# Graph layer on one core: gathers listed ahead in fours, steps joined, a new first part, placing one turn earlier

## The chip, the core and the metric

The kernel runs on one core of one Trainium2 chip. TensorE (PE; its weight loads are PEld), VectorE (DVE), ScalarE (ACT), GpSimd (POOL) and SyncE (SP) each work through a queue of their own in order and wait for one another by semaphores. The metric is the device time of one execution in microseconds.

## What is computed

One layer of a graph network over 12500 nodes of 128 features and 400000 edges, sorted by their target node `dst`; the edge type is 0 or 1:

```python
Xs = X[src]
m_data = Xs @ W_data.T + b_data
m_ctrl = Xs @ W_control.T + b_control
msg = jnp.where((edge_types == 0)[:, None], m_data, m_ctrl)
agg = jax.ops.segment_sum(msg, dst, num_segments=X.shape[0])
out = agg + (X @ W_self.T + b_self)
return jax.nn.relu(out)          # x = layernorm(x + this)
```

## The kernel before

The sums over edges are taken of the rows of x, apart by type, and multiplied by the weights afterwards. x is split into three bf16 parts that add up to the f32 value (`x3` in SBUF, `rows3` in DRAM, 3 x 128 columns a row).

The edges are 3125 chunks of 128. They make 25 groups of 125 chunks, and a group has four parts (`NE`). Each part is a run of 11 or 12 chunks that are **gathered** (kind "p") and a run of 20 chunks that are **picked** (kind "e").

- *Gathered*: for each chunk POOL gathers 128 rows of `rows3` by an indirect DMA (L700, tile `msg`), and TensorE adds them to their nodes by three products with a 0/1 matrix `psel` and one product that counts (L658, L712). `msg` has 24 buffers (`AHEAD`).
- *Picked*: the rows come from SBUF. Each step brings 25 lots (`q`) of 128 rows. For each, four TensorE products with 0/1 columns (`pick`) copy rows of `x3` into the PSUM tile `got` (L732); two lots share a `got`, of which there are two. ScalarE copies it to `emsg` (L743, five buffers). Three products with `esel` then add the lot to its nodes (L658), and one counts (L761). Rows that don't fit go through one small indirect gather, tile `last` (L747), and an extra copy (L756).

`picked(w)` is one of 100 **steps**, seven units long: unit t < 6 makes the got of lots 4t to 4t+3, counts and adds the lots of the unit before; the seventh adds the last lots, runs what is tiled there, and accumulates. `esel` is made by VectorE in three goes (`choose`, two buffers). Where a step's sums end, `accumulate` (L682) loads a start column `place_i` into a register and adds the PSUM tile `sums` to `acc` in SBUF (L688). `sums` has two buffers, shared by gathered and picked.

What a step picks is worked out ahead. `give_slots(w+2)` runs within step w: the matrix `O` (VectorE), a product `before` (L537), `ranks` and `rank_matrix` (VectorE, up to `rv`), then `put` (L601, 20 products) and `spread` (copy `cell`, write `there`, and load it to all partitions as `pick`, on SP's queue) in unit 5, and `turn_codes` and `keep_codes` (L621, L489; copies L631, L496, L498, and L500, which makes `idx` for `last`) in unit 6. `pick_matrix` (L643) compares `pick` in place. `prep_e` and `prep_p` ready the index data of the next group; `finish` multiplies by the weights, normalises and writes out once a group is complete.

`merged` sorts units of several streams by a fraction of the step, and within the lists a scheduler still moves an instruction of an engine's queue ahead of others where it expects it to be ready earlier. The gathers of `msg` are issued where a chunk is used, and that scheduler moves them forward as far as the 24 buffers go.

The first part loads and splits x (`split_units`: L246 to L249), loads the weights on ScalarE's queue (L274, L275), builds tables, works out `near`, `place_i` and the start nodes `node0` from the first edges of all windows (`first_i`, eight small loads), and makes the slots of steps 0 and 1.

Of the kernel before, what the change touches and what calls it, by code (L numbers as in the profile page):

```python
# [46 lines left out]
AHEAD = 24  # L47
# [101 lines left out]
def short_path(ctx, tc, const, ident, eps, wT, brow, bad, x, src, dst, etype, ws, bs, out):  # L149
# [49 lines left out]
    first_i = keep.tile([1, NG, NWIN], I32, name="first_i")  # L199

    def load_first(kind):
        for i, (k, _, c, _) in enumerate(windows(0)):
            if k == kind:
                nc.sync.dma_start(
                    out=first_i[:, :, i:i + 1],
                    in_=dst.rearrange("(o g e) -> o g e", o=1, g=NG)[:, :, c * P:c * P + 1],
                )
# [65 lines left out]
    for i, (w, b) in enumerate(zip(ws, bs)):  # L273
        nc.scalar.dma_start(out=wn[:, i, :], in_=w)  # L274
        nc.scalar.dma_start(out=brow[:, i, :], in_=b.rearrange("(o d) -> o d", o=1))  # L275
# [61 lines left out]
    halves = tmp.tile([1, 2, NG * NWIN], I32, name="halves")  # L337
    nc.vector.memset(x3[:, NBLK - 1], 0.0)
    first = first_i.rearrange("o g w -> o (g w)")
    nc.vector.tensor_single_scalar(halves[:, 0, :], first, 7, op=OP.logical_shift_right)  # L340
    nc.vector.tensor_single_scalar(halves[:, 1, :], first, 127, op=OP.bitwise_and)
    halves_b = tmp.tile([1, 2, NG * NWIN], BF, name="halves_b")
    nc.vector.tensor_copy(halves_b, halves)
    fin0 = ps1.tile([P, 512], FP, name="fin")
    for i in range(2):
        nc.tensor.matmul(fin0[:, :NG * NWIN], scale[:, i, :], halves_b[:, i, :], start=(i == 0), stop=(i == 1))
    node0 = keep.tile([P, NG, NWIN], FP, name="node0")
    nc.vector.tensor_copy(node0, fin0[:, :NG * NWIN].rearrange("p (g w) -> p g w", w=NWIN))
    near = keep.tile([rows_p, NG], FP, name="near")
    from_i = tmp.tile([rows_p, 1], I32, name="from_i")  # L350
    from_f = tmp.tile([rows_p, 1], FP, name="from_f")
    nc.gpsimd.iota(from_i, pattern=[[0, 1]], base=-PAD, channel_multiplier=DPC)
    nc.vector.tensor_copy(from_f, from_i)
    for k in range(1, NE):
        ge = raw[f"ge{k}"] = tmp.tile([rows_p, 1], FP, name=f"ge{k}")
        nc.vector.tensor_scalar(
            ge, from_f, float(DPC * PB * k - PAD), float(-DPC * PB), op0=OP.is_ge, op1=OP.mult
        )
    for k in range(1, NE):
        nc.vector.tensor_add(from_f, from_f, raw.pop(f"ge{k}"))  # L360
    nc.vector.tensor_scalar(near, near_i, from_f, None, op0=OP.add)
    place = tmp.tile([1, 2, NG, NWIN], FP, name="place")
    ref = tmp.tile([1, NG, NE, 2], I32, name="ref")
    nc.gpsimd.iota(ref, pattern=[[GN, NG], [0, NE], [-PAD, 2]], base=PAD - M0, channel_multiplier=0)
    ref = ref.rearrange("o g e k -> o g (e k)")
    least = tmp.tile([1, NG, NWIN], FP, name="least")
    for i, (_, _, c, _) in enumerate(windows(0)):
        nc.vector.memset(least[:, :, i:i + 1], float(max(0, c * DPC - PAD)))
    nc.vector.tensor_tensor(place[:, 0], first_i, ref, op=OP.subtract)
    nc.vector.tensor_tensor(place[:, 1], place[:, 0], least, op=OP.max)  # L370
    nc.vector.tensor_scalar(place[:, 1], place[:, 1], float(R - WMAX), None, op0=OP.min)
    place_i = keep.tile([1, NG, NWIN], I32, name="place_i")
    nc.vector.tensor_copy(place_i, place[:, 1])
    nc.vector.tensor_tensor(place[:, 0], place[:, 0], place[:, 1], op=OP.not_equal)
    nc.vector.tensor_reduce(worst[0:1, 2, 0:1], place[:, 0].rearrange("o g w -> o (g w)"), AX.X, OP.max)

    wps = ps1.tile([P, 512], FP, name="fin")
    for i in range(3):
        nc.tensor.transpose(wps[:, i * D:(i + 1) * D], wn[:, i, :], ident)
    nc.scalar.copy(wT, wps[:, :3 * D].rearrange("p (i d) -> p i d", d=D))  # L380
# [36 lines left out]
    def prep_p(g):  # L417
# [6 lines left out]
        def first():  # L424
            nc.vector.tensor_copy(sf, s)
            nc.vector.tensor_scalar(rel, d, near[:, g:g + 1], None, op0=OP.subtract)
            codes["n", g] = code_of(rel, t, PW, 0, "p")
# [11 lines left out]
    def prep_e(g):  # L439
# [3 lines left out]
        for i in range(NE):  # L443
            cs = slice(i * EC, (i + 1) * EC)
            nc.vector.tensor_scalar(rel[:, cs], d[:, cs], node0[:, g, 2 * i + 1:2 * i + 2], None, op0=OP.subtract)
# [59 lines left out]
    def give_slots(w):  # L505
# [128 lines left out]
        s["tiled"] = {5: [put, spread], 6: [turn_codes, keep_codes]}  # L634
# [47 lines left out]
    def accumulate(g, i, ps, wide, width):  # L682

        begin_acc(g)
        with tc.issue_after(added[-2].ins) if len(added) > 1 else ExitStack():
            at = nc.vector.value_load(place_i[0:1, g, i:i + 1], min_val=0, max_val=R - WMAX)
        win = acc[g][:, :, bass.ds(at, width)]
        added.append(nc.vector.tensor_add(win, win, ps[:, :4 * wide].rearrange("p (a w) -> p a w", w=wide)[:, :, :width]))  # L688

    def gathered(g, i):  # L690
# [7 lines left out]
        def chunk(c):  # L698
            msg = mp.tile([P, 3 * D], BF, name="msg")
            nc.gpsimd.indirect_dma_start(  # L700
                out=msg, out_offset=None, in_=rows3[:, :],
                in_offset=bass.IndirectOffsetOnAxis(ap=codes["p", g][0][:, i * PB + c:i * PB + c + 1], axis=0),
            )
# [7 lines left out]
            add_rows(rows, msg, sel, c == 0, c == n - 1)  # L711
# [6 lines left out]
    def picked(w, tiled):  # L718
# [46 lines left out]

        def unit(t):

            if t < turns:
                for q in range(t * per, (t + 1) * per, pair):
                    rows(q)  # L770
            if t == 0:
                choose(0)
            if t == 1:
                choose(8)
                spare_rows()
            if t == 3:
                choose(16, 9)
            if 0 < t < turns:
                for q in range((t - 1) * per, t * per if t < turns - 1 else NQ):
                    count(q)  # L780
            if t < turns:
                for u in tiled.get(t, []):
                    u()
            if t == turns - 1:
                last_rows()
            if t > 0:
                for q in range((t - 1) * per, t * per if t < turns else NQ):
                    add_rows(cells_of(s["ps"], EW, 0), s["msg"].pop(q), s["sel"][q], False, q == NQ - 1)
            if t == turns:
                for u in tiled.get(t, []):  # L790
                    u()
                accumulate(g, 2 * i + 1, s["ps"], EW, EW)

        turns = (NQ - 1) // per
        return evenly([lambda t=t: unit(t) for t in range(turns + 1)])
# [106 lines left out]

    prep_e(0)
    merged(evenly(all_slots(0) + all_slots(1)), evenly(split_units))
# [5 lines left out]
    mp = ctx.enter_context(tc.tile_pool(name="msg", bufs=AHEAD))  # L910
# [6 lines left out]
    for u in prep_p(0):  # L917
        u()

# [8 lines left out]

    for w in range(pairs):
# [4 lines left out]
        if i == 2 and g + 1 < NG:  # L934
# [9 lines left out]
        if w + 3 < pairs:  # L944
            more += [(0.55, lambda: [u() for u in begin_slots(w + 3)])]
        merged(
            chunks.pop(w, []),
            picked(w, tiled),
# [3 lines left out]
            evenly(rest),  # L952
# [3 lines left out]
        for p in closed.pop(w, []):  # L956
# [5 lines left out]
            if gp == NG - 1 and ip in soon:  # L962
                rest += finish(gp, soon[ip])
    for u in rest:
        u()
# [158 lines left out]
```

## Time and profile before

| | us |
|---|---|
| median of 9 runs | 2422.44 |
| lowest, highest | 2406.81, 2442.39 |
| the profiled execution | 2432.58 |
| its span, first to last instruction | 2430.8 |
| mean granted clock of TensorE, as a share of full | 0.900 |

The page cuts the span into 40 slices. Each digit is the busy share in tenths; PEclk is the granted clock in tenths:

```profile
PE   0468887888878887887778777787887878888878
DVE  6747676666666676676666666666766665666753
ACT  3435555555545554555545554455554544555535
POOL 0356565666556666566556565566665565666561
PEclk9869899898888989999889998889998898999989
```

The first slice and a half are the first part; the steps run from about 77 us on, with the opening of the main loop in slices two and three; they are alike until the end.

Costly groups beside those shown further on (line, engine, operation; busy us, mean ns of one | idle of the engine before them, and who ended most of it):

```profile
L700 POOL DMA_INDIRECT msg<-rows,pidx x1125 | 1270.5, 1129 | 871.4 <-PE sums L658 430.9
L732 PE MATMUL got<-x,pick 128*32 128x384 bf16 x9800 | 669.4, 358 | 262.7 <-ACT emsg L743 179.0
L658 PE MATMUL sums<-esel,emsg 128*128 128x176 bf16 x7200 | 757.1, 257 | 49.9 <-issue 48.1
L463 DVE TENSOR_TENSOR esel<-code_col,code 128x1408 bf16<-128x1408 bf16 (+1 forms) x300 | 275.0, 917 | 372.7 <-PE sums L658 259.9
```

"issue" is idle time with no wait that the profile shows; "remote", or "another core or an unknown queue", is a semaphore event that it can't put down to an engine.

### The profile page before, as it was taken

To read this page: it belongs to the slowest core of one execution; us is meant where nothing else is said; L and a number is where in the kernel's file an instruction comes from. 1 tells how busy PE (TensorE), PEld (TensorE's weight loads), DVE (VectorE), ACT (ScalarE), POOL (GpSimd) and SP (SyncE) were. 2 spreads that over 40 slices of the span, in tenths; PEclk is the share of its full clock that TensorE was granted. 3 is DMA by queue.
4 is the path that set the end of the run, shared out by engine and by line. 5 is a ranking of instruction groups with operands and counts; after the bars stand their busy time and mean duration, and the time that the engine had idled before them with its cause. 6 is when DMAs were issued, how large, how long until landed. Compare 5 with 4: busy or idle time off the path is not lost.

```text
span 2430.8 us, 70786 instructions
## 1 busy us (share of the span) xinstructions
PE 1883.0 (77%) x28867; PEld 1380.9 (57%) x28867; DVE 1584.9 (65%) x4224; ACT 1231.3 (51%) x2322; POOL 1392.3 (57%) x1243
## 2 busy tenths in 40 slices
PE   0468887888878887887778777787887878888878
PEld 0246565656555665665556555565665656666646
DVE  6747676666666676676666666666766665666753
ACT  3435555555545554555545554455554544555535
POOL 0356565666556666566556565566665565666561
PEclk9869899898888989999889998889998898999989
DMA  7423343332333333333333332323323332333331
GB/s 205 143 75 106 93 110 89 96 104 82 100 81 103 105 88 99 106 85 104 102 87 94 88 100 84 104 83 102 104 84 98 87 95 82 104 97 104 83 98 41
DMA packets 185017, 236.73 MB, mean 97 GB/s; under 512 B 80295, under 2 KB 152282, under 8 KB 184682
## 3 DMA queue, kind: packets, MB, share of 16 engines
q0 software_dynamic: 57200, 115.59, 18.3%
q1 hardware_dynamic: 114418, 109.94, 14.5%
q10 hardware_dynamic: 13064, 6.60, 1.0%
q8 instruction: 228, 3.74, 0.7%
q14 instruction: 107, 0.88, 0.1%
HBM read 215.35 MB, written 16.64 MB: 95 GB/s over the span
## 4 chain that ended last, share of the span: by engine, by line
PE 63%; ACT 10%; issue 9%; DVE 7%; another core or an unknown queue 6%; DMA 3%; SPq 1%; POOL 0%; DVEq 0%; ACTq 0%; POOLq 0%
PE sums L658 30%; PE got L732 22%; ACT emsg L743 9%; PE fin L850 3%; PE rk L601 2%; PE sums L761 2%; PE rk L489 1%; PE sums L712 1%; DVE esel L463 1%; DMA xt<-in_x_dram 1%; PE rk L537 1%; DVE pick L643 1%; PE rk L621 0%; PE fin L837 0%
## 5 line engine op out<-in xcount | busy, mean ns | idle before, releaser
L700 POOL DMA_INDIRECT msg<-rows,pidx x1125 | 1270.5, 1129 | 871.4 <-PE sums L658 430.9
L743 ACT CAST emsg<-got 128x768 bf16<-128x768 f32 x1200 | 921.1, 803 | 837.9 <-PE got L732 357.1
L732 PE MATMUL got<-x,pick 128*32 128x384 bf16 x9800 | 669.4, 358 | 262.7 <-ACT emsg L743 179.0
L658 PE MATMUL sums<-esel,emsg 128*128 128x176 bf16 x7200 | 757.1, 257 | 49.9 <-issue 48.1
L658 PEld LDWEIGHTS <-emsg 128*128 128x128 bf16 x7200 | 587.8, 104 | 221.6 <-issue 217.9
L463 DVE TENSOR_TENSOR esel<-code_col,code 128x1408 bf16<-128x1408 bf16 (+1 forms) x300 | 275.0, 917 | 372.7 <-PE sums L658 259.9
L732 PEld LDWEIGHTS <-pick 128*32 128x32 bf16 x9800 | 244.8, 98 | 446.6 <-issue 360.2
L658 PE MATMUL sums<-psel,msg 128*128 128x48 bf16 x3375 | 243.0, 188 | 49.3 <-issue 36.5
L658 PEld LDWEIGHTS <-msg 128*128 128x128 bf16 x3375 | 191.5, 100 | 80.2 <-issue 74.1
L688 DVE TENSOR_TENSOR acc<-acc,sums 128x352 f32 (+1 forms) x200 | 94.0, 470 | 160.8 <-PE sums L658 50.7
L712 PE MATMUL sums<-psel,one_col 128*128 128x48 bf16 x1125 | 185.7, 186 | 16.7 <-issue 16.4
L747 POOL DMA_INDIRECT last<-rows,idx x100 | 117.8, 1178 | 139.8 <-DMA pdst<-in_dst_dram 91.8
L761 PE MATMUL sums<-esel,one_col 128*32 128x176 bf16 x2500 | 168.6, 257 | 16.4 <-issue 13.9
L463 DVE TENSOR_TENSOR O<-cell_col,blk 128x2000 bf16<-128x2000 bf16 x100 | 119.3, 1193 | 60.6 <-PE got L732 28.0
L643 DVE TENSOR_SCALAR pick<-pick,lane_f 128x1600 bf16<-128x1600 bf16 x200 | 126.2, 646 | 15.1 <-DMA pick<-there 14.8
L601 PE MATMUL rk<-rv,O 128*128 128x64 bf16 x2000 | 90.3, 198 | 56.0 <-DVE rv L589 35.0
L761 PEld LDWEIGHTS <-one_col 128*32 128x32 bf16 x2500 | 85.0, 105 | 66.6 <-issue 33.5
L712 PEld LDWEIGHTS <-one_col 128*128 128x128 bf16 x1125 | 110.2, 98 | 17.2 <-issue 16.9
L551 DVE TENSOR_TENSOR prod<-O,ahead 128x2000 bf16<-128x2000 bf16 x100 | 119.0, 1190 | 0.0
L547 DVE TENSOR_REDUCE ahead<-rk 128x100 bf16<-128x500 f32 x100 | 67.5, 675 | 76.1 <-PE got L732 50.8
L601 PEld LDWEIGHTS <-O 128*128 128x128 bf16 x2000 | 73.9, 101 | 74.3 <-issue 61.3
L631 ACT CAST code<-rk 128x50 bf16<-128x50 f32 x100 | 20.3, 203 | 184.2 <-PE got L732 81.6
(170 smaller groups left out, 1995.4 us busy)
## 6 DMA issues: line engine op xcount, KB each, us to landing
pick<-there SPq DMA_DIRECT2D x100, 800.0 KB
msg<-rows,pidx POOLq DMA_INDIRECT x1125
rows<-x SPq DMA_DIRECT2D x6, 1344.0 KB
xs<-in_x_dram SPq DMA_DIRECT2D x99, 62.5 KB
out_dram<-h SPq DMA_DIRECT2D x99, 62.5 KB
xt<-in_x_dram ACTq DMA_DIRECT2D x6, 896.0 KB
psrc<-in_src_dram SPq DMA_DIRECT2D x100, 6.0 KB
pdst<-in_dst_dram SPq DMA_DIRECT2D x100, 6.0 KB
```

The source lines that it names most:

```text
L463: nc.vector.tensor_tensor(sel.rearrange("p n (w t) -> p n w t", t=2), col[:rows].rearrange("p (o w t) -> p o w t", o=1, t=2).to_broadcast( ...
L551: nc.vector.tensor_tensor(prod, s["O"], ahead.rearrange("p (o j) -> p o j", o=1).to_broadcast([P, EC, NCELL]), op=OP.mult)
L601: nc.tensor.matmul(s["rk"][:m, :2 * CAP], s["held"][:, c * NCELL:c * NCELL + m], s["rv"][:, c].rearrange("p v r -> p (v r)"), start=(c == ...
L643: nc.vector.tensor_scalar(t, t, lane_f, None, op0=OP.is_equal)
L658: nc.tensor.matmul(out, msg[:, j * D:(j + 1) * D], sel, start=(start and j == 0), stop=stop, skip_group_check=True)
L688: added.append(nc.vector.tensor_add(win, win, ps[:, :4 * wide].rearrange("p (a w) -> p a w", w=wide)[:, :, :width]))
L700: nc.gpsimd.indirect_dma_start(out=msg, out_offset=None, in_=rows3[:, :], in_offset=bass.IndirectOffsetOnAxis(ap=codes["p", g][0][:, i * P ...
L712: nc.tensor.matmul(cnt, one_col, sel, start=False, stop=(c == n - 1), skip_group_check=True)
L732: nc.tensor.matmul(ps[CAP * a:CAP * (a + 1), :], slots[w]["pick"][:, a * NQ + q, :], x3[:, 4 * q + a - a0].rearrange("p j d -> p (j d)"), ...
L743: nc.scalar.copy(msg, ps[:, :, :3 * D])
L747: nc.gpsimd.indirect_dma_start(out=msg[:OVF, :], out_offset=None, in_=rows3[:, :], in_offset=bass.IndirectOffsetOnAxis(ap=slots[w]["idx"], ...
L761: nc.tensor.matmul(cells_of(s["ps"], EW, 1)[CAP * (q % 4):CAP * (q % 4 + 1), :], one_col[:, :CAP], s["sel"][q], start=(q < 4), stop=(q + 4 ...
```

## The change

Constants: gathers come in tiles of four chunks (`SB`), six such tiles (`HOLD`), five of them listed ahead.

```diff
-AHEAD = 24
+SB = 4
+HOLD = 6
+AHEAD = 5
...
+    def fetch():
+        if to_fetch:
+            g, i, c = to_fetch.pop(0)
+            msg = mp.tile([P, SB, 3 * D], BF, name="msg")
+            for k in range(min(SB, PC[i] - c)):
+                at = i * PB + c + k
+                nc.gpsimd.indirect_dma_start(
+                    out=msg[:, k, :], out_offset=None, in_=rows3[:, :],
+                    in_offset=bass.IndirectOffsetOnAxis(ap=codes["p", g][0][:, at:at + 1], axis=0),
+                )
+            fetched.append(msg)
...
         def chunk(c):
-            msg = mp.tile([P, 3 * D], BF, name="msg")
-            nc.gpsimd.indirect_dma_start(
...
-            )
+            if c % SB == 0:
+                fetch()
+                s["msg"] = fetched.pop(0)
...
-    mp = ctx.enter_context(tc.tile_pool(name="msg", bufs=AHEAD))
+    mp = ctx.enter_context(tc.tile_pool(name="msg", bufs=HOLD))
...
+    for _ in range(AHEAD):
+        fetch()
```

The last five stand after `prep_p(0)`, ahead of the first step, so the first two gathers of `last` now follow 20 gathers of `msg`. Since rows are fetched earlier, `prep_p(g + 1)` moves from the step of part 2 to that of part 1, which also holds `prep_e(g + 1)`.

Steps have six units. What was the seventh is `end`, and the next step calls it in its first unit, after its own first got and its first `choose`. The gather of `last` moves from unit 1 to unit 2, and the units of `finish` start at 0.1 of the step.

```diff
+        def add(q0, q1):
+            for q in range(q0, q1):
+                add_rows(cells_of(s["ps"], EW, 0), s["msg"].pop(q), s["sel"][q], False, q == NQ - 1)
...
         def unit(t):
...
+            for q in range(t * per, (t + 1) * per, pair):
+                rows(q)
+            if t in (0, 1):
+                choose(8 * t)
             if t == 0:
-                choose(0)
-            if t == 1:
-                choose(8)
+                ending()
+            if t == 2:
                 spare_rows()
...
+        def end():
+
+            add((turns - 1) * per, NQ)
+            for u in tiled.get(turns, []):
+                u()
+            accumulate(g, 2 * i + 1, s["ps"], EW, EW)
...
-        return evenly([lambda t=t: unit(t) for t in range(turns + 1)])
+        return evenly([lambda t=t: unit(t) for t in range(turns)]), end
...
+        units, ending = picked(w, tiled, ending)
         merged(
             chunks.pop(w, []),
-            picked(w, tiled),
+            units,
...
-            evenly(rest),
+            evenly(rest, 0.1),
```

`put` and `spread` go from the sixth unit to the fifth:

```diff
-        s["tiled"] = {5: [put, spread], 6: [turn_codes, keep_codes]}
+        s["tiled"] = {4: [put, spread], 6: [turn_codes, keep_codes]}
```

First part: `first_i` becomes two tiles, one per kind, and the start nodes need that of "e" alone; the weights and biases are loaded on SP's queue, behind the first loads there; the first piece of x is split ahead of `prep_e(0)`; what works out `near` and `place_i` and turns the weights is one function, listed at 0.97 of the first part.

```diff
-    first_i = keep.tile([1, NG, NWIN], I32, name="first_i")
+    first_i = {k: keep.tile([1, NG, NE], I32, name=f"first_{k}") for k in "ep"}
...
-        nc.scalar.dma_start(out=wn[:, i, :], in_=w)
-        nc.scalar.dma_start(out=brow[:, i, :], in_=b.rearrange("(o d) -> o d", o=1))
+        nc.sync.dma_start(out=wn[:, i, :], in_=w)
+        nc.sync.dma_start(out=brow[:, i, :], in_=b.rearrange("(o d) -> o d", o=1))
...
-    first = first_i.rearrange("o g w -> o (g w)")
+    first = first_i["e"].rearrange("o g w -> o (g w)")
...
+    def places_and_weights():
+        near = raw["near"] = keep.tile([rows_p, NG], FP, name="near")
...
+    split_units.pop(0)()
     prep_e(0)
-    merged(evenly(all_slots(0) + all_slots(1)), evenly(split_units))
+    merged([(0.97, places_and_weights)], evenly(all_slots(0) + all_slots(1)), evenly(split_units))
```

## The prediction

> **What bounds the kernel now.** I read the page first, then the list of waits, then one step boundary in order of time, then stretches with their granted clock. From the page (L743 and L631 are the two copies of ScalarE that matter; behind the bar stands the idle time before them):
>
> ```profile
> span 2430.8 us, 70786 instructions
> ...
> PE 1883.0 (77%) x28867; PEld 1380.9 (57%) x28867; DVE 1584.9 (65%) x4224; ACT 1231.3 (51%) x2322; POOL 1392.3 (57%) x1243
> ...
> PE 63%; ACT 10%; issue 9%; DVE 7%; another core or an unknown queue 6%; DMA 3%; SPq 1%; POOL 0%; DVEq 0%; ACTq 0%; POOLq 0%
> ...
> L743 ACT CAST emsg<-got 128x768 bf16<-128x768 f32 x1200 | 921.1, 803 | 837.9 <-PE got L732 357.1
> ```
>
> No engine is full. TensorE carries 63% of the chain but stands still for 23% of the span; 100 steps share some 2330 us, 23.3 us each. The groups view adds the code copy, and the list of waits says who holds whom (us, times, longest):
>
> ```profile
> L631 ACT CAST code<-rk 128x50 bf16<-128x50 f32 x100 | 20.3, 203 | 184.2 <-PE got L732 81.6 <-PE sums L658 56.8 <-PE rk L489 30.7
> ```
>
> ```profile
> POOL msg L700 <- PE sums L658: 430.9, 301, 13.1
> ...
> ACT emsg L743 <- remote: 199.6, 61, 15.6
> PE got L732 <- ACT emsg L743: 179.0, 213, 16.1
> ```
>
> ScalarE stands 1.84 us per step in front of the code copy; TensorE loses 179 us to emsg copies; the gathers wait for free buffers, and TensorE waits for gathers only 1.2 us in all. One boundary in order of time (start, length, then what; idle time before it in brackets):
>
> ```profile
> 1286.72 1.07 PE L658 MATMUL sums<-esel,emsg 128*128 128x176 bf16 x12
> ...
> 1288.98 0.20 ACT L631 CAST code<-rk 128x50 bf16<-128x50 f32 x1 [2.10 <-PE sums L712]
> ...
> 1289.67 0.80 ACT L743 CAST emsg<-got 128x768 bf16<-128x768 f32 x1 [0.38 <-ACT part L498]
> ...
> 1291.74 0.95 POOL L700 DMA_INDIRECT msg<-rows,pidx  x1 [0.30 <-issue]
> ...
> 1292.99 1.02 POOL L700 DMA_INDIRECT msg<-rows,pidx  x1 [0.30 <-issue]
> ...
> 1293.69 0.31 PE L658 MATMUL sums<-esel,emsg 128*128 128x176 bf16 x2 [0.81 <-issue]
> ...
> 1295.18 0.20 PE L658 MATMUL sums<-psel,msg 128*128 128x48 bf16 x1 [1.15 <-issue]
> ...
> 1295.30 1.50 ACT L743 CAST emsg<-got 128x768 bf16<-128x768 f32 x2 [3.77 <-remote]
> ```
>
> TensorE ends a step with its last sums while ScalarE idles 2.10 us, queued behind a code copy that needs those sums done; only then does it copy the next step's first got. Then TensorE halts twice without a wait (0.81 and 1.15 us), in a run of gathers 1.25 us apart. The stretches show the clock (after the comma: PEclk, DMA share, GB/s):
>
> ```profile
> 1290.70:1300.00 9.30, 6.47 (x83) 4.50 (x79) 4.71 (x9) 3.81 (x5) 4.59 (x5) 0.72 0.39 127
> 1300.00:1308.00 8.00, 7.10 (x125) 4.86 (x125) 6.00 (x20) 4.38 (x6) 5.51 (x5) 0.90 0.20 51
> ```
>
> ```profile
> 106.00:132.00 26.00, 4.89 (x44) 1.97 (x43) 6.31 (x16) 2.10 (x3) 19.90 (x21) 0.57 0.29 76
> ```
>
> The third row is the 24 gathers that open the main loop, in one run: TensorE works 4.89 of 26 us.
>
> **The change part by part**, against the profiled execution's 2432.6 us (span 2430.8 and 1.8 around it), which is 10 us or 0.4% above the median of nine.
>
> A, joined steps. No instruction is added. The last 15 sums of a step, turn_codes and the accumulation move behind the next step's first 16 got. In the order in which the changed instructions stand, two emsg copies come between the last and the code copy in 97 steps, where none did. They need 2 x 0.803 = 1.61 us and fit into the hole of 1.84: 97 x 1.61 = 156 us of copies leave the restart. TensorE can win what it waits for them: 179.0 less the 16.1 of the opening is 163 us, and at the least half of it belongs to the restart (in the step above 0.30 and 0.58 us follow it, 0.71 and 0.19 come later): 81. I take 110, nearer the lower end, since the hole was partly cover for other waits. The later code copies delay idx and the gather of last by a turn; that gather is listed a turn later too, and its rows are used three turns on, so nothing is charged.
>
> B, the clock. A mean of 0.900 between 0.5 and 1.0 (132 to 141 us and 1289 to 1290.7 us show 0.50 and 1.00) is 0.2 x 2430.8 = 486 us at half rate; the stretch from 100 to 141 (0.51, 0.57, 0.50) takes 37, leaving 449, or 4.5 per step, and 9.3 x 0.28 x 2 = 5.2 of it follows the boundary above. At TensorE's share of 77%, half of 449 is 173 us at stake. I take a third, 58 (bounds 0 and two thirds, 115), because the halts in gather runs stay, and slow stretches follow those too. The Trainium skill, TensorE: Matmul & The Clock Gate, "What's actually happening", says that the gate drops to half rate after an idle window of about 3.4 us, and that for modelling the ramp is under 1% of a span. By that 1%, B would be at most 24 us and the sum 102 instead of 136. The rows, with 4.5 us of half rate in each step, say more.
>
> C, first part. VectorE waits 5.46 us for first_i up to 19.07, then works off prep_e and the places; the first split stands at 28.82. Changed, prep_e needs only the first four loads and runs in that hole, and the split stands right behind psf (23.41): up to 5 us. ScalarE's later waits for xt (3.85 and 4.95) may eat it; the six weight issues (0.29 to 0.57 us, 2.4 together) now go ahead of group 1's loads on SP, and bias is needed tens of us later. I take 3 (0 to 5).
>
> D, the opening. Twenty gathers are listed ahead of the first two last: 20 x 1.25 = 25 us later for these, and TensorE needs the first at the end of step 0, now inside step 1. But in that run it works 4.89 of 26 us anyway, and the rest of the run is shorter by as much. Taken 0; bounds -8 and +20.
>
> E, placing a turn earlier. The 20 rk products mostly move in front of 16 got. At four boundaries rv ends 3.5, 2.3, 3.4 and 2.1 us before rk starts; 16 got are 0.83 us: covered. If the cover goes, 0.5 us a step, 50. On SP the write of there and the pick load come earlier, and the load then stands waiting for the step's last got, with index loads, xs and out queued behind it; all waits for pick sum to 14.8 us and for esrc to 9.8. Taken 0, bounds 0 and 50.
>
> F, prep_p a step earlier. Six VectorE operations (204, 277, 277, 280, 210, 274 ns: 1.52 us) join the step that holds prep_e, 25 times: 0 to 38 us; VectorE is 65% busy: 10. Spreading finish from 0.1 moves nothing that is waited for.
>
> G, a new wait. The next step's first counts reuse the bank that the accumulation (0.47 us) empties, and the joined accumulation comes close in front of them. Between stand turn_codes, 7 products for spares, got and gathered sums, over a microsecond; what is queued behind the counts is all of TensorE's next turn. An O of 1.19 us in VectorE's way could cost 0.3 a step: 0 to 30, taken 5.
>
> H, gathers by four. Same count, same depth (20 to 24 chunks), and no wait for rows exists to be removed (1.2 us): the listing ahead is worth nothing by itself. But runs of about two (1225 issues, over 500 waits for buffers) become 300 runs of four, some with last as fifth, and halts come in runs. Bounds: 0, and one more halt of 0.81 + 1.15 = 1.96 us in two further runs a step, 2 x 98 x 1.96 = 384. Pauses between runs grow as well, so I take 20. The Trainium skill, SBUF — State Buffer, "SBUF: two separate sides", holds that DMA and compute engines do not contend. By it H is 0 and the sum 156; 4.89 busy of 26 us is hard to square with that.
>
> Sum: -110 - 58 - 3 + 10 + 5 + 20 = -136, so 2297 for an execution like the profiled one, and 2422 - 136 = 2286 at the median.
>
> **The rivals.** *Gather runs decide* (slower): each tile released lets four gathers go at once, and TensorE halts in them. Price 98 x 1.96 = 192 us for each further halting run per step. The gain of 171 in A to C is used up at about one; the small terms, 15, on top give +36, 2458; two give 2650. For it: the opening run. Against: the same number of gathers, and longer rests.
>
> *VectorE sets the step* (no change): it is busy 15.8 us a step and waits for esel buffers 259.9 us; if its chain from ahead to rv decides, the restart's gain turns into waits for rv, and C alone stays: about 2420. Against: the 2.1 to 3.5 us of slack.
>
> *The clock stays up* (larger gain): A 156, B 115, C 5, D 8: 2138.
>
> **How the numbers follow.** The likeliest case has 0.55, from 2220 (A at 135, B at 99) to 2373 (A at 81, B at 0, the rest as taken); the larger gain 0.16 (2138 to 2220); no change 0.13 (2398 to 2447); gather runs 0.16 (2447 to 2650). 1%, or 24 us, is about what a measurement of this kernel can tell from no change. Faster 0.71, same 0.13, slower 0.16. The range 2190 to 2440 leaves out some 0.07 below and 0.13 above.
>
> **What would show it.** A: idle before the code copy from 184 to under 60 us, TensorE's wait for emsg from 179 to under 100. B: a mean clock of 0.92 or more. C: main loop some us earlier. E: waits of rk for rv beyond the opening's 35.0. G: waits of one_col counts for acc. H: TensorE's issue gaps within sums and got, and ScalarE's 199.6 us for an unknown releaser, must not grow; if they do by 150 us, I am wrong through H. If the code copy's idle falls and the time does not, I am wrong through VectorE.

## The result, and the profile after

The changed kernel takes 2625.43 us (median of 20 runs, 2603.87 to 2653.37) against 2426.65 of the kernel before beside it (62 runs): a ratio of 1.082, with a 95% interval of 1.0796 to 1.0845. It is slower by 199 us; 2286 was predicted. The profiled execution of after took 2634.19 us.

One thing about the series of runs has to be known for what follows: the same kernel before took 2390 to 2427 us in some series and 1969 to 1986 in others, once so and once so on the same chip, so every ratio below is against the kernel before of the same series, taken over the runs within 1.5% of their kernel's fastest, and "halting" and "running" name the two kinds of series, for a reason that the traces will give. The comparison was of the halting kind.

The page of after (L765 is the copy that was L743, L638 the code copy that was L631, L695 the accumulation that was L688, L544 the products of `before` that were L537):

```profile
span 2632.5 us, 69897 instructions
...
PE 1985.0 (75%) x28867; PEld 1426.4 (54%) x28867; DVE 1571.2 (60%) x4225; ACT 1223.1 (46%) x2322; POOL 1473.3 (56%) x1243
...
PE 53%; another core or an unknown queue 14%; issue 10%; ACT 9%; DVE 8%; POOL 2%; DMA 1%; SPq 1%; DVEq 0%; ACTq 0%; POOLq 0%
...
L695 DVE TENSOR_TENSOR acc<-acc,sums 128x352 f32 (+2 forms) x200 | 94.0, 470 | 471.7 <-PE sums L665 143.8
...
L544 PE MATMUL rk<-prod,ltri 128*128 128x125 bf16 x400 | 47.5, 252 | 123.0 <-ACT part L505 109.2
...
L638 ACT CAST code<-rk 128x50 bf16<-128x50 f32 x100 | 20.3, 203 | 182.2 <-remote 144.4
```

The work is the same to a per cent on VectorE and ScalarE; it is stretched. The granted clock fell from 0.900 to 0.869 in the mean. The idle time before the code copy, which the prediction wanted under 60 us, stays at 182.2, but its cause is new: "remote", a semaphore event that the profile can't place, where it was TensorE's got and sums. Its share of the chain went from 6% to 14%. The trace has the semaphore itself: in all 39 of these waits of the code copy it is one that TensorE raises, over 1.5 us after the record of its product has ended. L544 and the accumulation stand idle as they did not before; there these were

```profile
L688 DVE TENSOR_TENSOR acc<-acc,sums 128x352 f32 (+1 forms) x200 | 94.0, 470 | 160.8 <-PE sums L658 50.7 <-PE got L732 39.9 <-remote 36.9
...
L537 PE MATMUL rk<-prod,ltri 128*128 128x125 bf16 x400 | 41.2, 226 | 34.8 <-ACT part L498 20.5 <-DVE prod L530 5.3 <-PE got L732 5.2
```

and of the code copy's idle time 6.7 us, in one wait, went to "remote".

The list of waits of after (us, times, longest):

```profile
POOL msg L707 <- issue: 293.1, 905, 6.8
ACT emsg L765 <- remote: 249.0, 90, 8.3
ACT code L638 <- remote: 144.4, 39, 9.5
...
PE got L754 <- ACT emsg L765: 136.8, 160, 7.2
DVE acc L695 <- remote: 133.9, 30, 10.5
...
PE rk L544 <- ACT part L505: 109.2, 38, 8.8
...
POOL last L769 <- DVE idx L507: 81.8, 32, 9.1
```

TensorE's wait for emsg did fall, from 179.0 to 136.8. Against that, TensorE now waits 109.2 us at L544 for ScalarE's `part` (before, at L537: 20.5 in 27 times, at most 1.6). The reader should look at three of these lines together: code copy, part and idx are one chain, and L544 and the gather of `last` hang on its end.

Little of the loss is in the opening. The fifth step's products with `last` start at 213.1 us before and 214.6 after; those of the fourth to the eighth start between 5.3 us earlier and 9.5 later. From the sixth step to the 96th a step takes 23.39 us before and 25.45 after: 2.06 us, about 200 in 97 steps.

One such step, in order of time (start, length, then what; idle time before it in brackets):

```profile
444.69 0.39 PE L496 MATMUL rk<-bits_b,om 128*64 128x3 bf16 x7
...
445.31 0.34 PE L754 MATMUL got<-x,pick 128*32 128x384 bf16 x1
446.04 0.95 POOL L707 DMA_INDIRECT msg<-rows,pidx  x1 [0.30 <-issue]
...
449.07 0.52 DVE L695 TENSOR_TENSOR acc<-acc,sums 128x352 f32 x1 [7.04 <-remote]
...
451.05 0.95 POOL L707 DMA_INDIRECT msg<-rows,pidx  x1 [0.30 <-issue]
454.07 0.20 ACT L638 CAST code<-rk 128x50 bf16<-128x50 f32 x1 [9.46 <-remote]
...
454.41 0.15 DVE L507 SCALAR_TENSOR_TENSOR idx<-part 64x1 int32<-64x1 f32 x1 [4.81 <-ACT part L505]
454.43 0.59 PE L544 MATMUL rk<-prod,ltri 128*128 128x125 bf16 x4 [8.78 <-ACT part L505]
...
454.83 1.97 POOL L769 DMA_INDIRECT last<-rows,idx  x1 [2.84 <-DVE idx L507]
```

L496 holds the last products on the rk bank in front of the code copy, and by the trace they are through at 445.1. ScalarE has nothing else to do, and yet the copy starts at 454.07. In between the gathers go on in an unbroken run, 1.25 us apart, until 452.00, where `last` blocks GpSimd's queue because idx is missing. TensorE's semaphore is raised at 449.05, which starts the accumulation, and then not before 454.05, which starts the code copy. L544, which writes the same bank, waits 8.78 us. The stretches before and within (busy us of PE, PEld, DVE, ACT, POOL with counts, then granted clock, DMA share, GB/s) show TensorE at work for 0.15 of 8.90 us beside six gathers:

```profile
436.00:445.50 9.50, 7.53 (x115) 5.55 (x111) 5.54 (x20) 4.97 (x9) 7.67 (x7) 0.82 0.51 150
445.50:454.40 8.90, 0.15 (x1) 0.11 (x1) 0.52 (x1) 0.31 (x3) 4.97 (x6) 0.75 0.28 75
```

How often that happens can be counted from the traces: the code copies that start 2 us or more after both their last product (by its end in the trace) and ScalarE's work before.

```
kernel (kind of series)               times of 100    us    longest
before (halting)                            5        16.7     5.89
after (halting)                            36       127.9     8.99
codes_in5 (halting)                        16        46.1     3.56
codes5_no_gathers_c (halting)               4        13.7     6.95
after_third, the change again (running)     0         0.0     0.20
```

In all 36 cases of after at least three gathers start from 3 us before the copy could go until it goes.

### The profile page after: what moved, and what is told of

Same layout as the page of the kernel before. It is cut to its first block, busy times and chain, and to the rows that moved or that the text cites. A ratio compares the mean times of both kernels' runs of the same rounds, so it can differ in the third digit from the quotient of the medians.

```text
span 2632.5 us, 69897 instructions
## 1 busy us (share of the span) xinstructions
PE 1985.0 (75%) x28867; PEld 1426.4 (54%) x28867; DVE 1571.2 (60%) x4225; ACT 1223.1 (46%) x2322; POOL 1473.3 (56%) x1243
## 4 chain that ended last, share of the span: by engine, by line
PE 53%; another core or an unknown queue 14%; issue 10%; ACT 9%; DVE 8%; POOL 2%; DMA 1%; SPq 1%; DVEq 0%; ACTq 0%; POOLq 0%
PE sums L665 22%; PE got L754 19%; ACT emsg L765 7%; PE fin L877 3%; PE rk L608 2%; POOL msg L707 2%; PE sums L783 2%; PE rk L544 1%; PE rk L496 1%; DVE esel L470 1%; PE sums L733 1%; DVE prod L558 1%; DVE rv L596 1%; DVE pick L650 1%
## 5 line engine op out<-in xcount | busy, mean ns | idle before, releaser
L707 POOL DMA_INDIRECT msg<-rows,pidx x1125 | 1321.8, 1175 | 1003.1 <-PE sums L665 413.4
L765 ACT CAST emsg<-got 128x768 bf16<-128x768 f32 x1200 | 918.1, 802 | 832.2 <-PE got L754 468.6
L754 PE MATMUL got<-x,pick 128*32 128x384 bf16 x9800 | 743.2, 365 | 257.3 <-ACT emsg L765 136.8
L665 PE MATMUL sums<-esel,emsg 128*128 128x176 bf16 x7200 | 802.2, 263 | 53.6 <-issue 51.3
L665 PEld LDWEIGHTS <-emsg 128*128 128x128 bf16 x7200 | 608.7, 107 | 265.7 <-issue 252.4
L695 DVE TENSOR_TENSOR acc<-acc,sums 128x352 f32 (+2 forms) x200 | 94.0, 470 | 471.7 <-PE sums L665 143.8
L665 PE MATMUL sums<-psel,msg 128*128 128x48 bf16 x3375 | 230.3, 190 | 33.0 <-issue 27.0
L783 PE MATMUL sums<-esel,one_col 128*32 128x176 bf16 x2500 | 192.3, 258 | 40.1 <-issue 34.1
L769 POOL DMA_INDIRECT last<-rows,idx x100 | 147.5, 1475 | 120.5 <-DVE idx L507 81.8
L783 PEld LDWEIGHTS <-one_col 128*32 128x32 bf16 x2500 | 95.8, 104 | 93.1 <-issue 68.5
L544 PE MATMUL rk<-prod,ltri 128*128 128x125 bf16 x400 | 47.5, 252 | 123.0 <-ACT part L505 109.2
L544 PEld LDWEIGHTS <-ltri 128*128 128x128 bf16 x400 | 31.4, 108 | 144.8 <-remote 107.5
L638 ACT CAST code<-rk 128x50 bf16<-128x50 f32 x100 | 20.3, 203 | 182.2 <-remote 144.4
```

Of the source, the lines that this page charges most:

```text
L544: nc.tensor.matmul(cols[:, :, cells], ltri[:, a, :], s["prod"][:, 2 * CQ:3 * CQ, cells], start=(a == 0), stop=(a == 3), skip_group_check=True,
L665: nc.tensor.matmul(out, msg[:, j * D:(j + 1) * D], sel, start=(start and j == 0), stop=stop, skip_group_check=True)
L707: nc.gpsimd.indirect_dma_start(out=msg[:, k, :], out_offset=None, in_=rows3[:, :], in_offset=bass.IndirectOffsetOnAxis(ap=codes["p", g][0] ...
L754: nc.tensor.matmul(ps[CAP * a:CAP * (a + 1), :], slots[w]["pick"][:, a * NQ + q, :], x3[:, 4 * q + a - a0].rearrange("p j d -> p (j d)"), ...
L765: nc.scalar.copy(msg, ps[:, :, :3 * D])
L769: nc.gpsimd.indirect_dma_start(out=msg[:OVF, :], out_offset=None, in_=rows3[:, :], in_offset=bass.IndirectOffsetOnAxis(ap=slots[w]["idx"], ...
```

## The experiments

First the four parts, each alone on the kernel before; then the change with one part taken out or one thing altered; then what these left open. Medians are in us, ratios carry their 95% interval.

**Each part alone.** only_join is the joined steps with six turns:

```diff
-        return evenly([lambda t=t: unit(t) for t in range(turns + 1)])
+        return evenly([lambda t=t: unit(t) for t in range(turns)]), end
```

> The kernel before with the joined steps alone (six turns, the end of a step run inside the first turn of the next, spare gather a turn later); gathers of one chunk, 24 buffers, the old placing and the old first part. Theory (the joined end): the code turning now stands right in front of the transposes that rebuild the one rk bank, so TensorE waits there for ScalarE's part copies, and the late idx holds POOL's queue; this run alone then carries most of the loss, 2540 to 2650 us, with ScalarE's part copies named as what TensorE's rk waits for (109 us after the whole change, 20 before). Rival (tiles of four): without them the joined steps gain, 2300 to 2400 us, as the prediction's steps A and B had it. If the parts only hurt together, it is 2420 plus or minus 25.

only_gathers and only_gathers_b are tiles of four, five listed ahead, with `prep_p` a step earlier, which belongs to it:

```diff
-AHEAD = 24
+SB = 4
+HOLD = 6
+AHEAD = 5
...
-        if i == 2 and g + 1 < NG:
+        if i == 1 and g + 1 < NG:
             more += evenly(prep_p(g + 1), 0.1, 0.7)
```

> The kernel before with the gathers listed five tiles of four chunks ahead alone (and the slot preparation a step earlier, which goes with it). Theory (the joined end): the gathers alone cost little, 2410 to 2470 us, with runs of four gathers but no blocked queue. Rival (tiles of four): runs of four halt TensorE, 2540 to 2650 us, and the time shows as slow products in runs of gathers, not as waits for part copies.

only_first is the new first part:

```diff
+    split_units.pop(0)()
     prep_e(0)
-    merged(evenly(all_slots(0) + all_slots(1)), evenly(split_units))
+    merged([(0.97, places_and_weights)], evenly(all_slots(0) + all_slots(1)), evenly(split_units))
```

> The kernel before with the new first part alone. Both theories: 2415 to 2424 us against 2422, -5 to 0 as the prediction's step C; the main loop begins some microseconds earlier.

only_place is the placing:

```diff
-        s["tiled"] = {5: [put, spread], 6: [turn_codes, keep_codes]}
+        s["tiled"] = {4: [put, spread], 6: [turn_codes, keep_codes]}
```

> The kernel before with the placing (put, spread) in the turn of index 4 instead of 5, alone. Both theories: within 1% of before, 2400 to 2446 us. If it costs, it does so as waits of TensorE's rk products for VectorE's rv (35 us before, nearly all in the opening), at most 50 us.

Measured, with the kernel before at 1983.54: only_join 2081.45, which is 1.049 (its four runs spread from 2045.61 to 2094.97, the lowest being 1.031, and no interval was given); only_gathers 2004.39, 1.010 (1.0072 to 1.0128); only_first 1977.24, 0.9955 (0.9915 to 0.9995); only_place 2039.66, 1.0264 (1.0198 to 1.0331). The joined steps looked like the culprit and the gathers nearly free. These four ratios add up to 1.081, but that this is the 1.082 of the comparison is luck: in a running series the whole change takes 1.027, as will be seen. The kernel before had been 2427 there, so this series could not be a picture of the comparison. The waits of only_first, which stands 0.4% from the kernel before, show the difference (us, times, longest):

```profile
PE sums L663 <- DMA last<-rows,idx: 178.0, 48, 13.4
POOL msg L705 <- issue: 138.3, 454, 0.3
...
POOL msg L705 <- PE got L737: 77.1, 253, 0.3
```

No gather of msg waits over 0.3 us: GpSimd issues one after the other without end, and what TensorE waits for most is the gather of `last`. From 400 to 1400 us the kernel before of the comparison and only_first compare so, in that order:

```profile
400.00:1400.00 1000.00, 808.40 (x12426) 591.88 (x12424) 666.46 (x1782) 516.61 (x985) 601.07 (x536) 0.90 0.34 96
```

```profile
400.00:1400.00 1000.00, 878.18 (x15321) 668.37 (x15321) 813.43 (x2186) 629.03 (x1219) 798.55 (x662) 0.94 0.41 118
```

In the same time TensorE gets through 15,321 products instead of 12,426. Halts can be counted too: products of one kind that start over 0.22 us apart with no wait between them, from 200 us to 50 before the end. The kernel before of the comparison has 255 us of them, 140 in halts over 0.6 us; only_first has 28, and none over 0.6. So in a running series TensorE does not halt for longer than 0.6 us beside an unbroken row of over a thousand gathers, and in a halting one it does beside runs of a few.

In a halting series the halts lie by the gathers. Call a run the gathers with under 0.45 us between two. Of the halts over 0.6 us, 90% in the kernel before and 99% in after lie between the start of the third gather of a run and 1 us behind its end, in 35% and 53% of the time. The packets that load instructions, 228 and 227 of them, lie on 14% and 13% of these halts, where the same halts moved at random would meet 20% and 17%, so they do not explain them. What puts a series into the one or the other stays open: chip 3 gave one of each.

**One thing taken out of the whole change.** after_again is the change as it is; no_join and no_place leave one part out; codes_in5 moves the code turning from the joined end to the last turn of the step before it:

```diff
-        s["tiled"] = {4: [put, spread], 6: [turn_codes, keep_codes]}
+        s["tiled"] = {4: [put, spread], 5: [turn_codes, keep_codes]}
```

> The whole change once more, unchanged, beside the runs of this call: on the chip of the single parts the kernel before takes 1984 us, where it took 2427 in the comparison, so ratios are what can be carried over. The single parts there: joined steps 1.05, placing 1.026, gathers 1.01, first part 0.996. If the parts add up, 1.07 to 1.09 on any chip; if the loss of the comparison came from TensorE's halts in runs of gathers, which the single-part traces hardly show (30 to 50 us of slow products against 250 to 320), it is 1.00 to 1.05 on a chip without them.

> The whole change but for the joined steps. Theory (the joined end carries most): 0.04 to 0.06 under after_again, so 1.02 to 1.04 over before. If the loss sits in the mix of parts, under 1.01 or over 1.06.

> The whole change but for the placing, which is again in the turn of index 5. If the placing's 2.6% come from rk products that wait for VectorE's rv, they stay with joined steps, and this is 0.02 to 0.03 under after_again. If the joined end hides them (rv waits of 17 us after the change against 35 before), it is within 0.01 of after_again.

> The whole change with the code turning (turn_codes, keep_codes) in the step's last turn (index 5) instead of in the joined end. Theory (late code turning): TensorE's wait of L544 for part copies (109 us after) falls under 20, idx comes before the next step, the gather of last no longer holds POOL, and the time falls by 0.03 to 0.06 against after_again. Rival (the restart itself, the sums and the accumulation in front of the next step): within 0.01 of after_again, and slower codes in the last turn would make it higher.

This series was a halting one, with before at 2423.22. after_again took 2622.98, 1.0819 (1.0729 to 1.0908). no_join took 2651.86, 1.0924 (1.0803 to 1.1044): with the other parts in place the joined steps are no loss, and the theory of the joined end falls in that form. no_place took 2615.77, 1.0787 (1.068 to 1.0894), within 0.01 of the whole, though the intervals are as wide as that. codes_in5 took 2543.10, 1.0502 (1.0407 to 1.0597): 80 us less than after_again beside it. Its groups show where from:

```profile
L544 PE MATMUL rk<-prod,ltri 128*128 128x125 bf16 x400 | 46.9, 242 | 13.0 <-issue 6.6 <-DVE prod L537 5.9 <-ACT code L638 0.3
...
L638 ACT CAST code<-rk 128x50 bf16<-128x50 f32 x100 | 21.0, 210 | 69.5 <-remote 47.3 <-PE got L754 12.5 <-PE sums L665 3.6
```

L544 no longer waits for `part` (95.0 us in after_again), and the code copy idles 69.5 instead of 171.0. That is the expected cause and the expected size. The wait of `last` for idx, which the theory also wanted gone, stays (81.8 us in after):

```profile
POOL last L769 <- DVE idx L507: 90.9, 29, 6.7
```

So it was not what the 80 us came from. And 1.05 is still a loss, with the gathers as the only part not yet taken out.

**Without the gathers.** no_gathers is the whole change with the gathers of before; codes5_no_gathers is the same with codes in the last turn, so that it differs from codes_in5 by the gathers alone. ahead_by_one keeps the listing ahead, but by single chunks, and codes5_ahead_by_one does that with the early codes:

```diff
-SB = 4
-HOLD = 6
-AHEAD = 5
+SB = 1
+HOLD = 24
+AHEAD = 20
```

> The whole change but for the gathers, which are again listed one chunk at a time where they are used, with 24 buffers. With the joined steps left out the whole change stayed at 1.09 and without the placing at 1.08, where the kernel before takes 2423 us. Theory now (gathers: the rival of the prediction, TensorE halts in runs of gathers): 0.99 to 1.02. Theory of the joined end: 1.05 to 1.08. Where the kernel before takes about 1984 us, as in the series of single parts, the sum of those parts says 1.07 for this one, and the two theories are not told apart.

> The gathers alone once more, since in their first series the kernel before took 1984 us and TensorE hardly halted. Theory (gathers): 1.06 to 1.10 where before takes 2423, 1.01 again where it takes 1984. Theory of the joined end: 1.01 in both.

> The whole change, but the gathers are listed 20 chunks ahead in tiles of one chunk (24 buffers), so that each buffer set free lets one gather go. If the runs of four are what costs: 0.99 to 1.03. If it is the listing ahead (gathers in front of last in GpSimd's queue, and last that waits there for idx with gathers behind it): 1.07 to 1.09, as the whole change.

> First part, placing and joined steps with the code turning in the last turn (index 5), gathers as before. The code turning there took 3.2% off the whole change. If gathers and code turning add up: 0.95 to 0.99, faster than the kernel before. If the early codes only mended what the gathers broke (last waiting for idx in front of a long row of gathers): as no_gathers, within 0.01.

A running series (before 1973.69): no_gathers 2034.63, 1.0297 (1.024 to 1.0354); only_gathers_b 1998.92, 1.0119 (1.0066 to 1.0172); ahead_by_one 2035.40, 1.0281 (1.0211 to 1.0351); codes5_no_gathers 1985.86, 1.0091 (1.0049 to 1.0132). The question was for halting series, and only the early codes are told apart: they take off about 2% here as well. So the same kernels went in again, with the change as an anchor.

> The whole change as an anchor for the three beside it. Where the kernel before takes about 2425 us: 1.08 as twice before. Where it takes about 1980: both theories say 1.03 to 1.05 there, the sum of no_gathers (1.03) and only_gathers (1.01); near 1.08 would mean that TensorE's halts, nearly absent there, aren't needed for the loss.

> The whole change but for the gathers, again. Where before takes about 2425: the theory that the gathers carry the half that early codes did not give back (codes_in5 1.05) says 1.00 to 1.04; the theory that all of it comes from the joined end and the placing says 1.07 to 1.09. Where before takes about 1980: 1.03 again.

> The whole change with gathers listed 20 chunks ahead in tiles of one, again. Where before takes about 2425: runs of four as the cause say 1.00 to 1.04 (as no_gathers_b); the listing ahead as the cause says 1.07 to 1.09. Where before takes about 1980: 1.03 again.

> First part, placing and joined steps with code turning in the last turn, gathers as before, again. Where before takes about 2425: if early codes (-0.03 on the whole change) and gathers as before add up, 0.97 to 1.01; if early codes only mend what the gathers broke, as no_gathers_b. Where before takes about 1980: 1.01 again.

Again a running series (before 1968.81): after_third 2028.61, 1.0274 (1.0208 to 1.034); no_gathers_b 2030.19, 1.0305 (1.0234 to 1.0376); ahead_by_one_b 2043.39, 1.0297 (1.0181 to 1.0412); codes5_no_gathers_b 1984.62, 1.0063 (1.002 to 1.0105). For halting series these say nothing, but the anchor tells something: the same change that costs 8.2% in a halting series costs 2.7% in a running one, the gathers add nothing to the rest there (alone they cost 1.0 and 1.2%), and the placing and joined steps, 2.6% and 3.1 to 5.6% alone, do not add up. The waits of after_third (its profiled run lies 0.9% above its median):

```profile
POOL msg L707 <- issue: 286.2, 939, 0.3
...
PEld L665 <- DMA last<-rows,idx: 187.5, 45, 19.0
ACT code L638 <- PE rk L496: 178.7, 71, 7.3
```

Past the opening, where one stands for 89.9, no gather waits over 2.3 us, no "remote" holds the code copy, and TensorE has no halt over 0.6 us.

> The whole change without the gathers and with the code turning in the last turn, a third time, for the state of the comparison: it differs from codes_in5 (1.05 there) by the gathers alone. Where before takes about 2425: if the gathers carry what is left, 0.98 to 1.01; if the joined steps, the placing or the first part carry it, 1.03 to 1.06. Where before takes about 1970: 1.01 for the third time, and the question stays open.

This one fell into a halting series (chip 2, before 2389.95): 2296.76, a ratio of 0.9654 (0.9559 to 0.9748), under the 0.98 to 1.01 that was expected of it. It is faster than the kernel before, by some 83 us: its slowest run took 2299.71, the fastest of the kernel before 2360.81. Against codes_in5 it is 0.0848 lower; the two intervals, of 0.0095 each, make 0.0134 on that difference. The two stand in different series on different chips, each against its own kernel before, and each was measured in one series only. The page and the groups of this run:

```profile
span 2297.9 us, 70748 instructions
...
PE 1833.2 (80%) x28867; PEld 1357.6 (59%) x28867; DVE 1571.0 (68%) x4225; ACT 1224.3 (53%) x2322; POOL 1440.5 (63%) x1243
...
PE 65%; DVE 12%; issue 11%; ACT 6%; another core or an unknown queue 4%; DMA 1%; DVEq 0%; POOL 0%; ACTq 0%; POOLq 0%
...
L738 PE MATMUL got<-x,pick 128*32 128x384 bf16 x9800 | 678.7, 349 | 171.3 <-ACT emsg L749 80.7
```

```profile
L636 ACT CAST code<-rk 128x50 bf16<-128x50 f32 x100 | 21.2, 212 | 34.3 <-PE sums L663 18.0 <-remote 11.0 <-PE got L738 2.5
```

The code copy idles 34.3 us (184.2 before), TensorE waits 80.7 for emsg (179.0), and the mean clock is 0.922: all three bounds that the prediction set for its steps A and B are met. TensorE's issue gaps and ScalarE's "remote", which the prediction watched for H, are in codes_in5

```profile
ACT emsg L765 <- remote: 290.6, 96, 6.5
...
PE got L754 <- issue: 118.3, 224, 2.7
...
PE sums L665 <- issue: 106.0, 250, 1.2
```

and in codes5_no_gathers_c

```profile
ACT emsg L749 <- remote: 108.2, 34, 19.9
...
PE got L738 <- issue: 74.3, 180, 2.1
...
PE sums L663 <- issue: 58.4, 135, 2.1
```

How gathers stand in GpSimd's queue, counted as runs from 200 us to 50 before the end, with the halts as above:

```
kernel                runs of 4 or more   mean run   halts, us   of these over 0.6 us
before                      121             2.84        255          140
codes5_no_gathers_c         110             3.50        261          113
codes_in5                   184             4.92        443          251
after                       163             5.18        361          193
```

Between codes_in5 and codes5_no_gathers_c lie 74 runs of four or more and 182 us of halts outside any wait, of a difference in the spans of 237. The halts are not the whole of it: codes_in5 has more of them than after and is faster, since in after late results also stand as waits at the code copy and at L544.

> Stands between codes_in5 (1.05) and codes5_no_gathers_c (0.965), which differ by the gathers alone: the gathers are listed 20 chunks ahead, but in tiles of one chunk (24 buffers). If the tiles of four are what costs (a buffer set free lets four gathers go, and TensorE halts in the run), 0.96 to 0.99 where before takes about 2400. If the listing ahead costs (the 20 chunks in front of the first last, and the slot preparation a step earlier), 1.03 to 1.06. Where before takes about 1970, 1.00 to 1.02 by both, and the two stay together.

A running series (chip 7, before 1985.70): 1991.81, 1.0021 (0.9998 to 1.0045). It was to tell tiles of four from the listing ahead, and did not: in a running series neither costs. So it is shown, by one pair of series, that the gathers, with the `prep_p` that goes with them, carry some 8.5%, and that TensorE's halts grow with them. That the halts come from runs of gathers rests on where they lie; by what mechanism is open. That it is the four at a time rather than the 20 ahead is only argued, from the runs in the table.

## Why the prediction was wrong

In halting series the change comes apart into three: everything but the gathers, with early codes, 0.9654; the gathers on top, +0.0848; the code turning in the joined end, +0.0317 (1.0819 less 1.0502). On 2427 us these are -84, +206 and +77, together +199, as measured; they add up by construction, since each is the difference of two neighbours. By the intervals each may be off by some 20 to 35 us.

**H failed, and most of the miss is there.** "Pauses between runs grow as well, so I take 20", of bounds 0 and 384. It measured 206, on top of the rest with early codes. The row behind it was the right one, and the rival *gather runs decide* had both mechanism and price: one further halting run of 1.96 us per step, 192 us. The prediction counted 300 runs of four in place of runs of about two, and set the longer pauses against them. By the traces the mean run went from 2.84 to 5.18, not to 4; that waits in front of GpSimd's queue join several tiles to one run is likely, and not shown. Its own sign for H would not have caught it in the change: TensorE's issue gaps within sums and got and ScalarE's wait for an unknown releaser make 362 us before (89.8, 72.7, 199.6) and 429 after (78.8, 101.6, 249.0), 67 more where 150 were asked. The late results stand elsewhere there, at the code copy and the accumulation: 144.4 and 133.9 us for "remote" instead of 6.7 and 36.9. Between codes5_no_gathers_c and codes_in5 the same sum goes from 241 to 515; runs of four or more grow by 74 and halts by 182 us there, so that the price of 192 is near by its size and not by its count of 98 runs. The Trainium skill, SBUF — State Buffer, "SBUF: two separate sides", holds that DMA and engines can't contend. It would have made H 0. The running series give no reason to doubt it (28 us of halts in only_first beside an unbroken row of gathers). In the halting ones TensorE worked 0.15 us of 8.90 beside six gathers; whether such a halt arises at SBUF no run shows, so the page is not refuted, but H could not be put at 0 by it.

**A had the right gain and left out a debt.** Its mechanism is there in codes5_no_gathers_c, where TensorE's wait for emsg falls by 98 us and 110 was taken. In the change it is not, by the sentence "The later code copies delay idx and the gather of last by a turn; that gather is listed a turn later too, and its rows are used three turns on, so nothing is charged." Followed was idx; what was not followed is the rk bank. With the code turning in the next step's first unit, the code and part copies stand directly in front of L544, which writes the bank that they read. Moved forward, it gave back 77 us of 2427. The debt is not apart from H: L544's wait for `part` is 109.2 us where results come late, and in after_third, the same kernel in a running series, `part` holds it nowhere. Early codes took off 2.1 and 2.4% in running series too, where they cut the code copy's idle time from 204.8 us (no_gathers) to 1.7 (codes5_no_gathers). Part of the 77 may be a gain that the kernel before would have had as well: early codes were not tried on it, nor were joined steps with late codes and the gathers of before in a halting series.

**G named the wrong bank.** It looked for a new wait of the counts for the sums bank; the counts (L783) have 5.1 us of waits for acc in all, as taken (1.7 before, at L761). The new wait was at rk, 109.2 us instead of 20.5. A wait for a bank that is used again has to be looked for at every bank whose reader was moved, not only at the one that the moved instruction itself empties.

**B** went the other way: by the mean clock, an estimate of 690 us at half rate after (2 x 0.131 x 2632.5) against 486 before; without the gathers and with early codes 358. That the clock follows the halts is inferred, from these three. A, B, C and G were -166; the same set, with the codes earlier, measured -84.

**C was a little more than given, and D lies within its bounds.** The first got starts at 70.6 us instead of 77.1, 6.5 earlier where 0 to 5 was given, and only_first is 0.45% faster, by an interval that ends at 0.05%. The six weight issues add up to 2.2 us in the trace, not 2.4, and nothing hangs on it. TensorE waits once, 21.2 us, for the first `last` behind the 20 gathers, but by the fifth step it is only 1.5 us late, as D had it. Since C had put it 6.5 ahead and the steps scatter by several us, D's 0 itself is not shown.

**E held where it was predicted, as far as the intervals tell.** no_place is within 0.01 of after_again, and rk's waits for rv fell from 35.0 to 17.0. In a running series the cover is smaller: only_place cost 2.6%, and its rk waits 61.8 us for rv, against 25.5 in only_first.

**F** was not tried by itself; it is within the gathers' share. *VectorE sets the step* was not the case in halting series: with the hole closed, the time fell.

The range ended at 2440, under the whole of that rival (2447 to 2650), whose chance was put at 0.16. Its price for two further halting runs, 2650, is the nearest number on record, but by luck: with 206 us for the gathers one such run would have been enough, and the rest was the debt in A.

The change with early codes and the gathers of before is the best version found for a halting series (0.965), and 0.6 to 0.9% slower than the kernel before in a running one; the new first part alone was the only one below 1 there.

## What to carry to other kernels

When an instruction is moved later, list every buffer that it reads and find who writes that buffer next: the price stands there, not only with those who use its result. Where a trace shows an engine halting beside another's work, price a change that bunches that work by the halting row, not by the count of instructions, and give that case the weight the row has. And measure parts in the series they are to explain: the gathers cost 1.0 to 1.2% where the kernel before ran at 1980, and some 8.5% where it ran at 2400.

## What the runs showed of the hardware

TensorE's results can reach other engines late while GpSimd issues a run of indirect DMAs: by more than 2 us 36 times in 100 steps of the change, at most 8.99, and never over 0.20 for the same kernel in a running series. The trace files it under "remote": TensorE's semaphore rises long after the product's record ends. These ends are modelled, so the trace can't tell whether the product itself ran late.

The same kernel, and the same chip, have two lasting speeds apart by 22% (1983.54 and 2423.22 on chip 3, in two series). In the faster one no halt over 0.6 us was found in TensorE (only_first, after_third), the clock is 0.94 instead of 0.90, GpSimd's gathers go back to back, and what TensorE waits for most is the gather of `last`. A single gather takes about as long in both (median 0.95 us before, 0.97 in only_first). What sets the speed was not found.
